# A decoder layer on one core: the attention's first unit of scores placed in front of the last projected block

## The chip, the core and the metric

The kernel runs on one core of a Trainium2 chip. The metric is the device time of one execution in microseconds (us); lower is better. The kernel before takes 804.1 us, the median of three executions (803.87 to 805.67). A difference of some 0.2% (1.6 us) is about what the measurement can tell from none.

## What is computed

A decoder layer in float32 on x[4, 512, 512] with a context[4, 512, 512], 16 heads of 32:

```python
x = x + self_attention(layernorm(x))        # causal; q, k, v, o projections with biases
x = x + cross_attention(layernorm(x), ctx, ctx)   # causal; no projections: keys = values = context
h = layernorm(x)
x = x + relu(h @ W_up.T) @ W_down.T + sum(softmax(top2(h @ W_gate.T))) * (h @ W_expert)
```

Both attentions are softmax(q k^T / sqrt(32)) v under a causal mask. The softmax subtracts each row's maximum, so the kernel forms the scores twice: once to find the maxima, and once, transposed and with the maxima subtracted, for the exponentials.

## The kernel before, in words

**Stages.** The four batches b = 0 to 3 are worked one after the other. Each has a self attention (stages s0 to s3), a cross attention (c0 to c3) and a feed-forward part. The 16 heads are four groups g of four heads. Besides, each attention stage has *fill*: projections of a neighbouring part, which give TensorE something to do while the maxima are found. A fill matmul (128x128 weights, 512 columns, float32) is two TensorE instructions. Four of them make a block of 128 rows or columns of a result. The fill is queries, keys and values of batch 0 in s0; up and down projections of batches 0 and 1 in s1 and s2; queries and keys of the next batch in c0, c1 and c2, with the expert blocks of batch 0 behind them in c1; expert blocks of batch 1 and two up blocks of batch 2 in s3; four down blocks of batch 2 in c3.

**Maxima.** `with_maxima` (L905) emits ten units of narrow score matmuls (32 rows of weights, `Attention.maxima`, L293), here called M1 to M10. Each unit fills two PSUM pairs, ScalarE copies them out (L304, two copies of 1024 columns), POOL masks the diagonal (L312), VectorE reduces to maxima (L324), and after the last unit of a group `split` (L341 to L350, VectorE) cuts the maxima into three bfloat16 parts. Between the units come the fill matmuls, shared out by a running due; a unit's VectorE jobs are emitted one by one behind the fill matmuls of the next gap. `rows` (L352) transposes a group's parts on TensorE (tiles `mt`, L361) and copies them to SBUF (`mrow`, L367); in cross attention `masked_sums` and `masked` (tiles `mb`, `ct`) do the like for fully masked keys.

**Scores and values.** `attend` (L954) then emits ten units of transposed scores (L405, with the maxima subtracted by the bfloat16 matmuls of L416), here sc0 to sc9: (g,0), then (g,3)+(g,1), then (g,2)+(g+1,2), then (g+1,0), then (g+1,3)+(g+1,1), twice. Each takes two PSUM pairs; ScalarE takes the exponential (L439, two of 1024 columns), POOL masks (L447), VectorE adds up the sums of the softmax (L552), and `values` multiplies with v (L482, tiles `pv`, one PSUM pair for the whole of a group). In the kernel before, `values` of the first unit (pv0) comes behind sc2. Behind sc3 come the transposes of the remaining maxima (`mt_..._both`).

**What sets the order.** The order of instructions on TensorE, VectorE, ScalarE and POOL is the order in which the code emits them (`tc.manual_schedule`). Each engine works its queue in order. PSUM is one pool of four pairs (L63 to L67); a new tile takes a pair once the reader of its last tile has released it. So a late reader on ScalarE or VectorE stops TensorE at the next tile that takes this pair.

**Evacuations.** Two blocks share a PSUM pair and are evacuated together, in one VectorE add of 1024 columns for v (`value`, L685) and down (`down`, L843), two weighted adds for the expert blocks (`weigh`, L867, each followed by a store on SP's queue), one ScalarE relu for up, and two ScalarE activations for queries and keys (`query_key`).

## Time and profile before

| what | us |
| --- | --- |
| median of three executions | 804.1 |
| their range | 803.87 to 805.67 |
| span of the profiled execution, first to last instruction | 803.7 |
| TensorE busy | 794.0 |
| VectorE busy | 565.9 |
| ScalarE busy | 395.2 |
| POOL busy | 339.6 |
| TensorE waits named in the trace, all | 5.7 |

The four named waits of TensorE are 2.4 us for the first layernorm, 1.5 us for the identity matrix, and 0.9 us each in the scores of the self and of the cross attentions (four times 0.2 us each), for exponentials. TensorE's queue can stand still for longer than these rows say: matmuls are pipelined, their recorded ends are modelled, and a stop shows as a longer distance between two starts. So the starts in the timeline are what to read. Busy times are averages over stages that differ: VectorE has long idle stretches at the start of a stage and is full at its end.

### The profile page before, as it was taken

What the parts mean: (1) busy time and instruction counts of PE and PEld (TensorE: products, weight loads), DVE (VectorE), ACT (ScalarE), POOL (GpSimd) and SP (SyncE); (2) the same over time, 40 slices, a digit from 0 to 9 for tenths busy, and PEclk for the clock granted to TensorE, in tenths of its full rate; (3) what the DMA queues carried; (4) which work ended last, traced back from release to release, by engine and by line L of the source; (5) the groups of instructions that cost most, each with busy time, mean ns of one, the idle gap of its engine ahead of it and who ended that gap; (6) DMA issues with size and microseconds to landing.
All of it is one profiled execution on the core that took longest, in us unless ns stands there. A gap on an engine that the chain in (4) does not pass through costs nothing.

```text
span 803.7 us, 13927 instructions
## 1 busy us (share of the span) xinstructions
PE 794.0 (99%) x5588; PEld 378.9 (47%) x5592; DVE 565.9 (70%) x963; ACT 395.2 (49%) x448; POOL 339.6 (42%) x523
## 2 busy tenths in 40 slices
PE   8999999999999999999999999999999999999998
PEld 6444454444444454444544455444444444444544
DVE  2378855889679854678867786588959766988512
ACT  2457516871456615567055742687156833674110
POOL 3434612564234732257332482256423652475100
PEclk9999999999999999999999999999999999999999
DMA  9710000001010000021100000000102000000101
GB/s 301 275 28 1 2 1 1 2 27 54 1 27 2 2 0 1 2 78 55 53 14 14 1 2 0 1 1 2 53 28 80 2 1 1 1 2 1 53 1 52
DMA packets 15282, 24.51 MB, mean 30 GB/s; under 512 B 2033, under 2 KB 5361, under 8 KB 15217
## 3 DMA queue, kind: packets, MB, share of 16 engines
q1 hardware_dynamic: 14496, 22.96, 8.6%
q8 instruction: 44, 0.72, 0.4%
q10 hardware_dynamic: 720, 0.66, 0.2%
q14 instruction: 22, 0.17, 0.1%
HBM read 19.42 MB, written 4.19 MB: 29 GB/s over the span
## 4 chain that ended last, share of the span: by engine, by line
PE 95%; ACT 2%; issue 1%; DMA 1%; DVE 0%; ACTq 0%
PE pm_qk L241 14%; PE pm_d L229 7%; PE pm_u L241 7%; PE pm_v L229 7%; PE pm_o L725 7%; PE pm_e L229 7%; PE pv_c L482 6%; PE pv_s L482 6%; PE sm_c L293 6%; PE sm_s L293 6%; PE sc_s L405 5%; PE sc_c L405 5%; PE sc_s L416 1%; PE sc_c L416 1%; PE tp_a L255 1%
## 5 line engine op out<-in xcount | busy, mean ns | idle before, releaser
L324 DVE TENSOR_REDUCE nm_s<-s_s 128x2 f32<-128x1024 f32 (+3 forms) x128 | 96.9, 810 | 34.7 <-POOL s_s L312 34.7
L324 DVE TENSOR_REDUCE nm_c<-s_c 128x2 f32<-128x1024 f32 (+3 forms) x128 | 95.8, 810 | 31.0 <-POOL s_c L312 31.0
L304 ACT COPY s_s<-sm_s 128x1024 f32<-128x1024 f32 x80 | 77.1, 1015 | 70.7 <-PE sm_s L293 36.7
L304 ACT COPY s_c<-sm_c 128x1024 f32<-128x1024 f32 x80 | 77.1, 1016 | 35.9 <-PE sm_c L293 16.2
L312 POOL TENSOR_SCALAR_AFFINE_SELECT s_c<-s_c 128x512 f32<-128x512 f32 (+1 forms) x80 | 43.9, 550 | 100.4 <-ACT s_c L304 100.4
L312 POOL TENSOR_SCALAR_AFFINE_SELECT s_s<-s_s 128x512 f32<-128x512 f32 (+1 forms) x80 | 43.8, 551 | 94.4 <-ACT s_s L304 94.4
L552 DVE TENSOR_TENSOR sum_s<-sum_s,pt_s 128x256 f32<-128x256 f32 (+2 forms) x72 | 59.9, 897 | 15.4 <-PE pv_s L482 15.4
L439 ACT ACTIVATE pt_c<-sc_c 128x1024 f32<-128x1024 f32 x64 | 61.7, 1031 | 18.1 <-PE sc_c L416 10.1
L447 POOL TENSOR_SCALAR_AFFINE_SELECT pt_c<-pt_c 128x512 f32<-128x512 f32 (+1 forms) x64 | 52.9, 833 | 20.7 <-ACT pt_c L439 20.2
L229 PE MATMUL pm_d<-wdown_sb,hT 128*128 128x512 f32 x128 | 61.5, 611 | 0.0
L241 PE MATMUL pm_qk<-xnT,wk_sb 128*128 128x512 f32 x128 | 61.0, 606 | 0.0
L241 PE MATMUL pm_u<-fT,wup_sb 128*128 128x512 f32 x128 | 59.3, 605 | 0.0
L439 ACT ACTIVATE pt_s<-sc_s 128x1024 f32<-128x1024 f32 x56 | 53.9, 1030 | 10.5 <-POOL pt_s L447 5.5
L229 PE MATMUL pm_v<-wv_sb,xnT 128*128 128x512 f32 x128 | 58.8, 600 | 0.0
L725 PE MATMUL pm_o<-wo_sb,oT_s 128*128 128x512 f32 x128 | 57.8, 596 | 0.0
L405 PE MATMUL sc_c<-cqT,ckT 32*128 32x384 f32 (+3 forms) x512 | 56.4, 464 | 0.9 <-ACT sum_c L439 0.9
L241 PE MATMUL pm_qk<-xnT,wq_sb 128*128 128x512 f32 x120 | 56.7, 605 | 0.0
L229 PE MATMUL pm_e<-wexp_sb,fT 128*128 128x512 f32 x120 | 56.3, 604 | 0.0
L447 POOL TENSOR_SCALAR_AFFINE_SELECT pt_s<-pt_s 128x512 f32<-128x512 f32 (+1 forms) x56 | 48.0, 865 | 16.9 <-ACT pt_s L439 16.2
L405 PE MATMUL sc_s<-qT,kT 32*128 32x128 f32 (+3 forms) x512 | 54.1, 464 | 0.9 <-ACT sum_s L439 0.9
L293 PE MATMUL sm_c<-ckT,cqT 32*128 32x512 f32 (+3 forms) x512 | 47.5, 460 | 0.0
L293 PE MATMUL sm_s<-kT,qT 32*128 32x512 f32 (+3 forms) x512 | 47.0, 461 | 0.0
(171 smaller groups left out, 1268.1 us busy)
## 6 DMA issues: line engine op xcount, KB each, us to landing
cv<-in_ctx_dram SPq DMA_DIRECT2D x16, 256.0 KB, 4.4
out_dram<-x SPq DMA_DIRECT2D x15, 256.0 KB, 2.0
xin<-in_x_dram SPq DMA_DIRECT2D x12, 256.0 KB, 2.8
x<-in_x_dram SPq DMA_DIRECT2D x12, 256.0 KB, 4.2
wq_sb<-in_wq_dram SPq DMA_DIRECT2D x2, 512.0 KB, 6.7
wk_sb<-in_wk_dram SPq DMA_DIRECT2D x2, 512.0 KB, 7.7
wv_sb<-in_wv_dram SPq DMA_DIRECT2D x1, 1024.0 KB, 7.8
wo_sb<-in_wo_dram SPq DMA_DIRECT2D x1, 1024.0 KB, 9.5
```

What stands on the lines that cost most here:

```text
L229: nc.tensor.matmul(pm, lhsT=lhs_t[:, c, t * P : (t + 1) * P], rhs=w[:, c, :], start=(c == 0), stop=(c == NC - 1),)
L241: nc.tensor.matmul(pm, lhsT=w[:, c, f * P : (f + 1) * P], rhs=rhs_t[:, c, :], start=(c == 0), stop=(c == NC - 1),)
L293: nc.tensor.matmul(scs[r // 2][:, r % 2, c : c + (i + 1) * P], lhsT=self.q_t[h, g, i * P : (i + 1) * P], rhs=self.k_t[h, g, : (i + 1) * P] ...
L304: nc.scalar.copy(s, scs[n])
L312: nc.gpsimd.affine_select(out=diagonal, in_=diagonal, compare_op=ALU.is_ge, fill=NEG, base=0, pattern=[[0, 2], [0, len(pieces)], [-1, P]], ...
L324: nc.vector.tensor_reduce(self.nm[g][:, i, 2 * n : 2 * n + 2], made[n][:, :, c : c + (i + 1) * P], axis=AX.X, op=ALU.max, negate=True,)
L405: nc.tensor.matmul(scs[r // 2][:, r % 2, c : c + S - j * P], lhsT=self.k_t[h, g, j * P : (j + 1) * P], rhs=self.q_t[h, g, j * P :], start= ...
L439: nc.scalar.activation(pt, scs[n], AF.Exp)
L447: nc.gpsimd.affine_select(out=diagonal, in_=diagonal, compare_op=ALU.is_ge, fill=0.0, base=0, pattern=[[0, 2], [0, len(pieces)], [1, P]], ...
L482: nc.tensor.matmul(pv[r * HD : (r + 1) * HD, u, j * P :], lhsT=ones if u else self.v[:, j, h * HD : (h + 1) * HD], rhs=pts[r // 2][:, r % ...
L552: nc.vector.tensor_tensor(to, to, pts[n][:, :, c : c + S - j * P], ALU.add)
L725: nc.tensor.matmul(pms[t // 2][:, t % 2, :], lhsT=a.out[:, c, t * P : (t + 1) * P], rhs=wo_sb[:, c, :], start=(c == 0), stop=(c == NC - 1),)
```

## The change

`with_maxima` keeps the last block of the fill apart (`last`). Its other blocks are shared out over the gaps between the ten maxima units (`merge=1`: nine gaps, so that nothing stands behind M10; `merge=0`: ten). Then it emits sc0, the first unit of scores, then the four matmuls of the last block, between them the VectorE jobs of M10, and then hands over to `attend`, which goes on with sc1. In c0, c1, c2, c3 and s3 (`merge=1`) sc0 follows M10 directly; in s0, s1 and s2 two or three fill matmuls still stand between. In s0 six fill matmuls instead of two lead, so that M1 has what it needs. `attend` multiplies the values of sc0 behind sc1 instead of behind sc2. The last block and the one before no longer share a PSUM pair in the stages' fills: each gets its own pair and is evacuated by itself. In c0 and c2 only the last key block gets a pair of its own, and its queries are evacuated ahead of it. In the stages where the copy of the third group's maxima stood in the last gap (c0, c1, c2) it now stands behind the second matmul of the last block.

```diff
     def query_key(e):
-        b, made = e.b, {}
+        b, made, apart = e.b, {}, (NC - 1,) if e.b % 2 else ()
...
         def query(f):
             made[f] = pair(f"pm_qk{b}_{f}")
             yield from project_t(made[f][:, 0, :], wq_sb, e.xn_t, f)
+            if f in apart:
+                out_query(f)
...
         def key(f):
-            yield from project_t(made[f][:, 1, :], wk_sb, e.xn_t, f)
-            out(f)
+            if f in apart:
+                pm = pair(f"pm_k{b}_{f}")[:, 0, :]
+            else:
+                pm = made[f][:, 1, :]
+            yield from project_t(pm, wk_sb, e.xn_t, f)
             nc.scalar.activation(
-                e.k_t[:, f, :], made[f][:, 1, :], AF.Identity, bias=bk_sb[:, f : f + 1]
-            )
+                e.k_t[:, f, :], pm, AF.Identity, bias=bk_sb[:, f : f + 1]
+            )
+            if f not in apart:
+                out_query(f)
...
         def one(t):
+            if b == 0 and t >= NT - 2:
+                pm = pair(f"pm_v{b}_{t}")[:, 0, :]
+                yield from project(pm, e.xn_t, wv_sb, t)
+                nc.vector.tensor_tensor(e.v[:, t, :], pm, bv_sb, ALU.add)
+                return
...
+            if b == B - 2 and f < 2:
+                pm = pair(f"pm_u{b}_{f}")[:, 0, :]
+                yield from project_t(pm, wup_sb, f_t, f)
+                nc.scalar.activation(made["h"][:, f, :], pm, AF.Relu)
+                return
...
         def down(t):
+            if t >= NT - 2 and b < B - 1:
+                pm = pair(f"pm_d{b}_{t}")[:, 0, :]
+                yield from project(pm, made["h"], wdown_sb, t)
+                if b == B - 2:
+                    aside(f"d{b}_{t}", t, pm)
+                else:
+                    nc.vector.tensor_tensor(e.x[:, t, :], pm, e.x[:, t, :], ALU.add)
+                return
...
         def expert(t):
...
+            if b == 0 and t >= NT - 2:
+                pm = pair(f"pm_e{b}_{t}")[:, 0, :]
+                yield from project(pm, f_t, wexp_sb, t)
+                weigh(t, pm, slice(0, D), nc.sync)
                 return
...
-    def with_maxima(steps, a, first=0, norms=()):
+    def with_maxima(steps, a, first=0, norms=(), merge=1):
...
+        fill, last = matmuls(steps[first:-1]), matmuls(steps[-1:])
+        total = sum(1 if step.__name__ in ("share", "gate") else NC for step in steps[first:-1])
+        early = total + NC >= 2 * len(units)
+
+        lead = 6 if first else 0
...
+        late = {3: NC - 1} if early else {3: 2, 5: NC - 1}
...
-            due += (total - lead) / len(units)
+            due += (total - lead) / (len(units) - merge)
...
-                if n == len(units) - 1 and k == count - (2 if count > 4 else 1):
-                    if total >= 2 * len(units):
-                        if a.cross:
-                            a.rows(2)[0](nc.scalar.copy)
-                    else:
-                        late = {3: 2, 5: NC - 1}
...
+        begun = [a.scores([(0, 0)])]
+        for k in range(NC):
+            next(last)
+            if k == 1 and a.cross and early:
+                a.rows(2)[0](nc.scalar.copy)
+            run(jobs[:1])
+            jobs = jobs[1:]
+        for _ in last:
+            pass
         run(jobs)
-        return late
+        return begun, late

-    def attend(a, late):
+    def attend(a, begun, late):
...
-        waiting, held, todo = [], [], []
+        waiting, held, todo = list(begun), [], []
...
-        for n, pieces in enumerate(units):
+        for n, pieces in enumerate(units[1:], 1):
             waiting.append(a.scores(pieces))
...
-            if len(waiting) > 2:
+            if n == 1 or n > 2:
                 values()
...
-            late = with_maxima(between_self, sa, skip, norms)
+            begun, late = with_maxima(between_self, sa, skip, norms, int(not more))
...
-            late = with_maxima(steps[3:], ca)
+            begun, late = with_maxima(steps[3:], ca)
```

More of the change, by code (lines that the diff above doesn't have):

```diff
@@ L638, in query, with out_query @@
             yield from project_t(made[f][:, 0, :], wq_sb, e.xn_t, f)
+            if f in apart:
+                out_query(f)
         def key(f):
-            yield from project_t(made[f][:, 1, :], wk_sb, e.xn_t, f)
-            out(f)
-        def out(f):
+            if f in apart:
[3 more added lines that the diff above has]
+            yield from project_t(pm, wk_sb, e.xn_t, f)
             nc.scalar.activation(
-                e.k_t[:, f, :], made[f][:, 1, :], AF.Identity, bias=bk_sb[:, f : f + 1]
+                e.k_t[:, f, :], pm, AF.Identity, bias=bk_sb[:, f : f + 1]
             )
+            if f not in apart:
+                out_query(f)
+        def out_query(f):
             nc.scalar.activation(
@@ L837, in down @@
             yield from project(made["d"][:, t % 2, :], made["h"], wdown_sb, t)
-            if t == NT - 1 and b == B - 2:
-                for n in range(2):
-                    aside(f"d{b}_{n}", t - 1 + n, made["d"][:, n, :])
-            elif t % 2 == 1:
+            if t % 2 == 1:
                 both = e.x[:, t - 1 : t + 1, :]
@@ L847, in expert @@
                 yield from expert_parts(t)
+                return
+            if b == 0 and t >= NT - 2:
+                pm = pair(f"pm_e{b}_{t}")[:, 0, :]
+                yield from project(pm, f_t, wexp_sb, t)
+                weigh(t, pm, slice(0, D), nc.sync)
                 return
@@ L903, in matmuls @@
             yield
-    def with_maxima(steps, a, first=0, norms=()):
-        norms = list(norms)
-        run(steps[:first])
-        fill = matmuls(steps[first:])
-        total = sum(1 if step.__name__ in ("share", "gate") else NC for step in steps[first:])
+    def with_maxima(steps, a, first=0, norms=(), merge=1):
         units = []
@@ L916, in with_maxima @@
             units += [u for k in (g, g + 1) for u in ([(k, 2), (k, 0)], [(k, NT - 1)])]
-        lead = 2 if first else 0
+        norms = list(norms)
+        run(steps[:first])
+        fill, last = matmuls(steps[first:-1]), matmuls(steps[-1:])
+        total = sum(1 if step.__name__ in ("share", "gate") else NC for step in steps[first:-1])
+        early = total + NC >= 2 * len(units)
+        lead = 6 if first else 0
         for _ in range(lead):
             next(fill)
-        done, due, jobs, late = lead, float(lead), [], {3: NC - 1}
+        late = {3: NC - 1} if early else {3: 2, 5: NC - 1}
+        done, due, jobs = lead, float(lead), []
         todo = []
@@ L1017, in decoder_layer @@
                 after, norms, turns = norm_in(b + 1)
-            late = with_maxima(between_self, sa, skip, norms)
+            begun, late = with_maxima(between_self, sa, skip, norms, int(not more))
             if b == B - 1:
                 e.x = load_x(b)
-            attend(sa, late)
+            attend(sa, begun, late)
             if b > 0:
@@ L1031, in decoder_layer @@
             ca.e, ca.out = e, e.beh_t
-            late = with_maxima(steps[3:], ca)
+            begun, late = with_maxima(steps[3:], ca)
             if b + 2 < B:
                 after.x = load_x(b + 1)
-            attend(ca, late)
+            attend(ca, begun, late)
             if more:
```

## The prediction

> **What bounds the kernel.** I read the page first, engines and then the chain of waits:

> ```profile
> PE 794.0 (99%) x5588; PEld 378.9 (47%) x5592; DVE 565.9 (70%) x963; ACT 395.2 (49%) x448; POOL 339.6 (42%) x523
> ...
> PE 95%; ACT 2%; issue 1%; DMA 1%; DVE 0%; ACTq 0%
> ```

> TensorE is nearly the whole chain, its granted clock is 9 (full) in every slice of the page, and the change keeps the number of its matmuls. So the only time to win is the few per cent in which TensorE's queue stands still, and the only time to lose is a new stop in it, or a change between the wide projections (128x128) and the narrow scores (32x128). Next I read TensorE's timeline where the first self attention begins (s0; columns: start, duration, instructions):

> ```profile
> 62.86 1.14 PE L293 MATMUL sm_s<-kT,qT 32*128 32x512 f32 x8
> 63.93 2.84 PE L229 MATMUL pm_v<-wv_sb,xnT 128*128 128x512 f32 x6
> 66.70 1.14 PE L405 MATMUL sc_s<-qT,kT 32*128 32x512 f32 x8
> ...
> 67.88 1.35 PE L405 MATMUL sc_s<-qT,kT 32*128 32x128 f32 x16
> ...
> 69.16 0.70 PE L405 MATMUL sc_s<-qT,kT 32*128 32x256 f32 x4
> 70.07 0.92 PE L405 MATMUL sc_s<-qT,kT 32*128 32x256 f32 x10 [0.21 <-ACT sum_s L439]
> ...
> 71.35 1.07 PE L482 MATMUL pv_s<-sum_s,v 128*32 128x512 f32 x8
> 72.35 1.17 PE L405 MATMUL sc_s<-qT,kT 32*128 32x512 f32 x6
> ...
> 74.10 0.62 PE L361 MATMUL mt_s_both<-identb,parts 128*128 128x128 bf16 x8
> ```

> M10 at 62.86, three fills (2.77), then sc0, sc1, sc2. sc2 starts at 69.16, stops after four matmuls and goes on at 70.07, when ScalarE's exponentials of sc0 have freed a PSUM pair. sc2 thus takes 2.19 (69.16 to 71.35) where the same shape undisturbed takes 1.38 (84.02 to 85.40); sc3 takes 1.75 (72.35 to 74.10) where 0.97 plus about 0.3 for the change to the transposes would do. Together about **1.3 us of stop** in a stage; in c0 about 1.7 (157.35 to 164.88). Eight stages of it are 11 to 12 us: all that the change can win. Then VectorE in the same stretch, because the new waits point there:

> ```profile
> 62.21 2.34 DVE L324 TENSOR_REDUCE nm_s<-s_s 128x2 f32<-128x1024 f32 x2
> ...
> 66.81 1.23 DVE L685 TENSOR_TENSOR v<-pm_v,bv_sb 128x1024 f32<-128x1024 f32 x1
> 67.95 1.27 DVE L324 TENSOR_REDUCE nm_s<-s_s 128x2 f32<-128x768 f32 x2
> 69.14 0.74 DVE L212 TENSOR_SCALAR xn_a<-xin,mv_a,rs_a 128x512 f32<-128x512 f32 x1
> 69.79 2.33 DVE L324 TENSOR_REDUCE nm_s<-s_s 128x2 f32<-128x1024 f32 x2
> ...
> 73.57 0.23 DVE L350 TENSOR_TENSOR parts<-rest_s,parts 128x16 bf16<-128x16 f32 x1
> ```

> VectorE is about 7 us behind TensorE: M10's scores were done at 63.9, their reductions run from 69.79, and the split of the last group ends at 73.80. The queue is solid from 57.1 on. In before nothing that TensorE needs early stands at its end.

> **The change, part by part.** (1) *Order.* Four projection matmuls (4 x 0.86 = 3.44 straight, 3.63 with the change of shape) stand between sc0 and sc1, so that sc0's two exponentials (1.94, row 68.08) run beside them. sc1 and the first half of sc2 then find their pairs. That is the gain. (2) *A new back-to-back.* values(sc0) now comes before sc2, so sc2 and sc3 follow each other and pv0 keeps a pair; sc3's second tile waits for the exponential of sc2's first tile: 0.97, with 0.2 until ScalarE starts (67.88 to 68.08) and as much until the scores are whole, less 0.5 for sc3's first tile that runs meanwhile. The trace has no such pair of units; the ends are 0.5 and 1.4, and I take a **0.95 stop** in every stage. So at best 1.3 - 0.95, some 0.35, is won, and in c0/c2 0.4 to 0.7. (3) *Changes of shape.* A unit between fills costs about 0.2 for each entry and exit (two fills take 1.92, where 2 x 0.86 is 1.72). In s0, s1, s2 M10 and sc0 stay apart, with one more pair of changes: +0.4 each, part of it hidden in the stop before. In the five stages in one visit the number of changes stays. (4) *Halved evacuations.* An add over 1024 columns takes 1.22 (L685), over 512 0.68 (L740): splitting adds 0.14 of VectorE, and frees the pair of block 2 earlier. (5) *A new wait at the end of a queue.* The last block has its own PSUM pair. With four pairs the turn comes round: by the waits of the built program sc2's first tile takes the pair of the last block. In s0, s1, s2 and c1 VectorE evacuates that block, and its add stands behind M10's reductions and the split. In c0, c2 (L648), s3 (relu) and c3 (the copy aside) it is ScalarE, which takes it in time (0.58 to 0.69). Behind the add on VectorE stand the L552 sums, and on TensorE sc2 holds up all else, as it works in order. The rest costs nothing: in c1 the stores on SP's queue are as many as before (one of 256 KB after each weighted add, median 2.0 us to land by the page) and no matmul waits for them; in c3 POOL's two put-off adds are the same two; ScalarE's copy of the third group's maxima (0.58) moves behind sc0's exponentials into a queue that has 1.9 free (354.54). If these covers failed, the copy alone would delay sc1's exponentials by 0.6.

> *s0.* Three fewer matmuls stand before M10: 62.86 - 2.58 = 60.3; M10 1.07, two fills 1.92: sc0 at 63.3; to the fills 1.18, last block 3.64: sc1 at 68.1; +1.46: pv0 69.6; +1.0: sc2 wants to start at **70.6**. VectorE: M8's reductions can start at 61.6 (0.6 earlier, the row idle at 57.1 closes), and the rest is 11.6 in before (62.21 to 73.80) - 1.23 + 0.68: split done at about 72.7, last add at **73.4**. sc2 stops for 2.8. Then 1.38, sc3's 0.97 + 0.95: the transposes at 76.7 instead of 74.10: **+2.6**. If the add came in time it would be -0.15.

> *s1, s2.* VectorE's rows, before:

> ```profile
> 250.05 1.22 DVE L843 TENSOR_TENSOR x<-pm_d,x 128x1024 f32<-128x1024 f32 x1 [1.25 <-PE pm_d L229]
> ...
> 253.03 2.33 DVE L324 TENSOR_REDUCE nm_s<-s_s 128x2 f32<-128x1024 f32 x2
> ```

> The 1.25 of waiting goes, as block 2 is done sooner, and M10 comes 3.4 earlier (four fewer matmuls before it). By the same steps sc0 is at 246.5, sc2 wants 253.8; VectorE's split ends at 253.7 to 254.6 (257.04 in before, less 1.25, less 0.5 to 0.7 for the halved add, less up to 0.9 of older idle time) and the add 0.7 later, 254.4 to 255.3. Stop 0.6 to 1.5; I take 1.2, transposes near 258.3 against 257.34: **+0.9** each; with the add in time -0.2.

> *c1.* As many matmuls stand before M10; sc0 follows at 350.6. Its second tile needs the pair of block 2, whose weighted add (0.70, half of the row of 1.41 at 354.31) now stands behind the split that ends at 350.99: done at 351.7, a stop of 1.3 where there is none now. Transposes near 362.7 against 361.83: **+0.9**; without the stop -0.4.

> *c0, c2.* sc0 follows M10 at 153.35, sc1 at 158.6, transposes 164.5 to 164.9 against 164.88: **-0.2** each.

> *s3, c3.* Two fewer matmuls before M10. If TensorE alone sets the pace, M10 is 1.7 earlier and the way from M10 to the transposes is 12.5 instead of 10.4 (s3) or 11.2 (c3): +0.4 (s3), -0.4 (c3). But c3's fills are as short as one matmul and VectorE is nearly full there; M10 itself is stretched to 1.98 (702.45) by its PSUM pair. If M10 can't move, it is +2.1 (s3) or +1.3 (c3). VectorE's slack in s3 is larger; I take 0 and **+0.3**, with the ends -0.4 and +1.5 for both.

> The sum: 2.6 + 0.9 + 0.9 + 0.9 - 0.4 + 0 + 0.3 = **+5.2 us**. The profiled span is 803.7, the median of the runs 804.1; the difference I carry over: **809.3**. With every cover in place: -0.15 - 0.4 - 0.4 - 0.8 - 0.8 = -2.5, so 801.6. With every end the other way (VectorE not ahead in s0: 3.3; s1, s2 1.5 each; c1 1.3; s3, c3 1.5 each) +10.6.

> [...]

> **Rivals.** *A, forecast:* the last block's add at the end of VectorE's queue holds sc2 in s0 to s2, and c1's sc0: 806 to 812. For: VectorE's solid rows. Against: the lag in s1/s2 is only about 1 us longer than the cover. *B, the other side:* the add comes in time, as VectorE gets its maxima earlier than I counted. In s0 VectorE must gain 2.8 us, in s1/s2 1.2, in c1 1.3; then only part 2's stop remains and the eight stages give -2.5: **801.6**, faster. For: M10's scores are 3 to 4 us earlier, and VectorE has free time ahead of them (3.32 us idle before 50.23); where ScalarE's copies set the start of the reductions, all moves ahead. Against: that idle time was ended by the transposes of the first group, which stay at about 50. *C, even:* the stops are there, but in s1, s2 and c1 no longer than what (1) gives: +2.6 - 0.2 - 0.2 - 0.4 - 0.8 = about +1 to -1: **804 to 805**. *D, worse:* c3 and s3 are held by VectorE and M10 doesn't move: **812 to 815**. *E,* that the change does not do what it says: sc0 is in front of the last block in the instruction lists, so I give it nothing.

> **The numbers.** A 0.63, B 0.18, C 0.13, D 0.06. Less than 0.2% (1.6 us) is about what a measurement of this kernel can tell from no change. Faster by more: B and little else, 0.19. Within: C, 0.13. Slower: A and D, 0.68. The likeliest is A at 809.3, its own range 806 to 812. For 8 in 10 I leave out D and the far end of B: 802.0 to 812.0.

> **What would show it.** In the profile after: in s0, between pv0 and sc2, TensorE idle or stretched for about 2.8 us, ended by VectorE's add of v, and the transposes near 76.7; in s1 and s2 the same of 1 us with the add of pm_d; in c1 sc0 stretched by 1.3. In every stage a stop of about 0.95 inside sc3, ended by the exponential of sc2. In c0 the transposes near 164.7. I am wrong if sc2 starts right behind pv0 in s0 (then B), if sc3 shows no stop (then the gain is up to 7 us larger), or if the loss is in c3 or s3.

## The result, and the profile after

The changed kernel takes 811.88 us (median of four executions, 810.52 to 813.52) against 804.03 us of the kernel before on the same chip; the ratio is 1.0092, with a 95% interval of 1.0075 to 1.0109. It is slower by 7.4 us by that ratio, by 7.9 us by the medians. The forecast was 809.3, its range 802.0 to 812.0.

The page of the changed kernel: TensorE does the same 5588 matmuls, and the span grows from 803.7 to 811.9.

```profile
PE 798.5 (98%) x5588; PEld 378.1 (47%) x5592; DVE 561.8 (69%) x966; ACT 396.4 (49%) x449; POOL 337.8 (42%) x523
```

TensorE's waits in the changed kernel (us in total, times, longest) name who held it:

```profile
PE sc_s L405 <- DVE v L691: 2.4, 1, 2.4
PE tp_a L255 <- DVE xn_a L212: 1.9, 1, 1.9
PE sc_c L405 <- ACT pt_c L439: 1.5, 4, 0.4
...
PE sc_s L405 <- ACT pt_s L439: 1.0, 3, 0.4
PE sm_s L293 <- ACT qT L655: 0.5, 1, 0.5
PE sc_c L405 <- DVE x L894: 0.2, 1, 0.2
```

The first row is the last block's add in s0, the last one the weighted add in c1, the `pt` rows are the stop between sc2 and sc3. TensorE's timeline of s0 in the changed kernel, to be laid beside the one in the prediction:

```profile
63.99 1.14 PE L405 MATMUL sc_s<-qT,kT 32*128 32x512 f32 x8
...
65.27 3.70 PE L229 MATMUL pm_v<-wv_sb,xnT 128*128 128x512 f32 x8
68.91 1.15 PE L405 MATMUL sc_s<-qT,kT 32*128 32x128 f32 x16
...
70.20 1.07 PE L482 MATMUL pv_s<-sum_s,v 128*32 128x512 f32 x8
73.63 1.62 PE L405 MATMUL sc_s<-qT,kT 32*128 32x256 f32 x16 [2.36 <-DVE v L691]
...
75.44 2.43 PE L405 MATMUL sc_s<-qT,kT 32*128 32x512 f32 x6
...
78.45 0.62 PE L361 MATMUL mt_s_both<-identb,parts 128*128 128x128 bf16 x8
```

pv0 ends at 71.27 and nothing runs until 73.63. VectorE in the same stretch shows why: the add of the last block of v stands behind M10's reductions and the split.

```profile
68.90 2.34 DVE L324 TENSOR_REDUCE nm_s<-s_s 128x2 f32<-128x1024 f32 x2
...
72.33 0.69 DVE L350 TENSOR_TENSOR parts<-rest_s,parts 128x16 bf16<-128x16 f32 x1
72.90 0.68 DVE L691 TENSOR_TENSOR v<-pm_v,bv_sb 128x512 f32<-128x512 f32 x1
```

**Where the 8 us came from.** In each stage I took the start of the last transposes of maxima in `attend` (the `mt` rows, 74.10 and 78.45 in s0), subtracted the same row of the kernel before, and from that the difference of the stage before. s0 is counted from the start of M1, less the 3.44 us of the four matmuls that now stand ahead of it. (In e4, e8 and e9 nothing is taken off, as s0 is that of the kernel before.) This leaves out the time up to M1, which differs by up to 2.2 us between profiled executions (the first layernorm ends TensorE's wait after 0.5 to 2.45 us) and also moves the totals. e5 has no row: its one profiled execution ran at a mean clock of 0.947, where the others have 0.996 to 1.000. Differences to the kernel before in us:

| kernel | s0 | c0 | s1 | c1 | s2 | c2 | s3 | c3 | ratio of times (95%) |
| --- | --- | --- | --- | --- | --- | --- | --- | --- | --- |
| changed | +4.40 | +1.44 | -0.22 | +1.17 | -0.22 | +1.43 | +0.19 | -0.01 | 1.0092 (1.0075 to 1.0109) |
| e1 jobs behind the add | +1.02 | +1.44 | -0.29 | +1.17 | -0.28 | +1.43 | +0.18 | -0.01 | 1.0053 (1.0041 to 1.0066) |
| e2 values as before | +4.79 | +1.02 | -0.32 | +0.62 | -0.32 | +0.89 | -0.40 | -0.33 | 1.0066 (1.0054 to 1.0079) |
| e3 both | +0.43 | +0.85 | -0.88 | +0.58 | -0.87 | +0.84 | -0.40 | -0.33 | 0.9990 (0.9981 to 0.9999) |
| e4 s0 as before | +0.01 | +1.48 | -0.23 | +1.18 | -0.23 | +1.43 | +0.18 | -0.01 | 1.0039 (1.0026 to 1.0053) |
| e6 fill and weigh | +0.43 | 0.00 | -0.88 | +3.50 | -0.88 | 0.00 | -0.40 | -0.32 | 1.0012 (1.0003 to 1.0020) |
| e7 busy in the stop | +3.38 | +1.43 | -0.22 | +1.17 | -0.22 | +1.43 | +0.19 | -0.02 | 1.0079 (1.0065 to 1.0092) |
| e8 all but s0 | +0.01 | +0.05 | -0.88 | +3.54 | -0.87 | -0.01 | -0.40 | -0.33 | 0.9989 (0.9980 to 0.9999) |
| e9 five stages | +0.01 | +0.02 | -0.88 | -0.54 | -0.88 | -0.05 | -0.40 | -0.31 | 0.9962 (0.9949 to 0.9975) |
| e10 apart everywhere | +0.44 | +1.71 | -0.88 | -0.03 | -0.88 | +1.72 | +1.12 | +0.93 | 1.0048 (1.0034 to 1.0062) |
| e11 together everywhere | +0.34 | +0.85 | +0.45 | +0.58 | +0.44 | +0.86 | -0.40 | -0.31 | 1.0023 (1.0013 to 1.0033) |
| e12 paired evacuations | +0.43 | +2.00 | -0.88 | +1.16 | -1.07 | +1.99 | +0.87 | +0.36 | 1.0055 (1.0041 to 1.0068) |

A stage that an edit leaves alone repeats to about 0.05 us from run to run (s0 as before: +0.01 three times; the other seven stages in the changed kernel, e4 and e7), so the table resolves more than the totals do. The expectations of e5, e6, e8 and e9 quote figures of the e3 row that are 0.2 to 0.3 higher in the cross stages and as much lower in s1, s2 and s3; by the definition above the figures are those of the table. Half of the loss is in s0, most of the rest in c0, c1 and c2; s1, s2, s3 and c3 are even.

### The profile page after: what moved, and what is told of

Same layout as the page of the kernel before. It is cut to its first block, busy times and chain, and to the rows that moved or that the text cites. A ratio compares the mean times of both kernels' runs of the same rounds, so it can differ in the third digit from the quotient of the medians.

```text
span 811.9 us, 13931 instructions
## 1 busy us (share of the span) xinstructions
PE 798.5 (98%) x5588; PEld 378.1 (47%) x5592; DVE 561.8 (69%) x966; ACT 396.4 (49%) x449; POOL 337.8 (42%) x523
## 5 line engine op out<-in xcount | busy, mean ns | idle before, releaser
L324 DVE TENSOR_REDUCE nm_s<-s_s 128x2 f32<-128x1024 f32 (+3 forms) x128 | 97.0, 810 | 36.6 <-POOL s_s L312 36.4
L324 DVE TENSOR_REDUCE nm_c<-s_c 128x2 f32<-128x1024 f32 (+3 forms) x128 | 95.7, 811 | 31.0 <-POOL s_c L312 31.0
L552 DVE TENSOR_TENSOR sum_s<-sum_s,pt_s 128x256 f32<-128x256 f32 (+2 forms) x72 | 59.5, 887 | 26.5 <-PE pv_s L482 21.9
L439 ACT ACTIVATE pt_c<-sc_c 128x1024 f32<-128x1024 f32 x64 | 62.0, 1021 | 24.5 <-PE sc_c L416 14.5
L439 ACT ACTIVATE pt_s<-sc_s 128x1024 f32<-128x1024 f32 x56 | 54.3, 1021 | 25.4 <-PE sc_s L416 14.7
L447 POOL TENSOR_SCALAR_AFFINE_SELECT pt_s<-pt_s 128x512 f32<-128x512 f32 (+1 forms) x56 | 50.3, 908 | 34.4 <-ACT pt_s L439 33.8
L229 PE MATMUL pm_d<-wdown_sb,hT 128*128 128x512 f32 x128 | 60.9, 609 | 0.0
L405 PE MATMUL sc_c<-cqT,ckT 32*128 32x384 f32 (+3 forms) x512 | 57.5, 460 | 1.8 <-ACT pt_c L439 1.5
L229 PE MATMUL pm_v<-wv_sb,xnT 128*128 128x512 f32 x128 | 58.9, 600 | 0.0
L405 PE MATMUL sc_s<-qT,kT 32*128 32x128 f32 (+3 forms) x512 | 54.4, 469 | 3.5 <-DVE v L691 2.4
L229 PE MATMUL pm_e<-wexp_sb,fT 128*128 128x512 f32 x120 | 56.5, 604 | 0.0
L241 PE MATMUL pm_qk<-xnT,wk_sb 128*128 128x512 f32 x112 | 53.6, 605 | 0.0
L293 PE MATMUL sm_c<-ckT,cqT 32*128 32x512 f32 (+3 forms) x512 | 50.5, 460 | 0.0
L293 PE MATMUL sm_s<-kT,qT 32*128 32x512 f32 (+3 forms) x512 | 46.5, 461 | 0.5 <-ACT qT L655 0.5
```

The lines of the kernel that those rows point to most:

```text
L229: nc.tensor.matmul(pm, lhsT=lhs_t[:, c, t * P : (t + 1) * P], rhs=w[:, c, :], start=(c == 0), stop=(c == NC - 1),)
L241: nc.tensor.matmul(pm, lhsT=w[:, c, f * P : (f + 1) * P], rhs=rhs_t[:, c, :], start=(c == 0), stop=(c == NC - 1),)
L293: nc.tensor.matmul(scs[r // 2][:, r % 2, c : c + (i + 1) * P], lhsT=self.q_t[h, g, i * P : (i + 1) * P], rhs=self.k_t[h, g, : (i + 1) * P] ...
L324: nc.vector.tensor_reduce(self.nm[g][:, i, 2 * n : 2 * n + 2], made[n][:, :, c : c + (i + 1) * P], axis=AX.X, op=ALU.max, negate=True,)
L405: nc.tensor.matmul(scs[r // 2][:, r % 2, c : c + S - j * P], lhsT=self.k_t[h, g, j * P : (j + 1) * P], rhs=self.q_t[h, g, j * P :], start= ...
L439: nc.scalar.activation(pt, scs[n], AF.Exp)
```

## The experiments

Theory Q was the forecast's: the last block's evacuation stands at the end of VectorE's queue and holds the PSUM pair of sc2. Rival B: the order sc2, sc3 back to back costs. Rival F, formed from the table: four matmuls kept back leave too little fill between the maxima in c0 and c2.

**e1: M10's VectorE jobs behind the last block.**

```diff
         for k in range(NC):
             next(last)
...
-            run(jobs[:1])
-            jobs = jobs[1:]
         for _ in last:
             pass
         run(jobs)
```

> As the changed kernel, but the VectorE jobs of M10 (two to four reductions and the split) are emitted behind the last block instead of between its matmuls, so the block's evacuation stands ahead of them in VectorE's queue. Theory Q (VectorE's queue holds the last block's PSUM pair): in s0 the add of v is done at about 69.6 instead of 73.5, sc2 starts directly behind pv0 (71.2 instead of 73.6), and the slower granted clock behind the stop (0.62 and 0.74 in the 5.4 us after it) goes too: 3 to 4 us less, all in s0; 808 to 809. Rival B (the back-to-back of sc2 and sc3 is what costs): the stop of 1.4 in sc3 stays in each of eight stages, the time stays at 811 to 812. Rival F (too little fill between the maxima): no change either, 811 to 812.

Measured: 809.51 us, ratio 1.0053. The time is half a microsecond above what Theory Q gave, the place is right: s0 falls by 3.38, and no other stage moves by more than 0.07. VectorE's timeline of e1 in s0 now has the add first:

```profile
69.12 0.69 DVE L691 TENSOR_TENSOR v<-pm_v,bv_sb 128x512 f32<-128x512 f32 x1
69.73 2.33 DVE L324 TENSOR_REDUCE nm_s<-s_s 128x2 f32<-128x1024 f32 x2
```

And in TensorE's timeline of e1 sc2 follows pv0 directly:

```profile
70.31 1.06 PE L482 MATMUL pv_s<-sum_s,v 128*32 128x512 f32 x8
71.31 1.31 PE L405 MATMUL sc_s<-qT,kT 32*128 32x256 f32 x16
...
73.91 0.70 PE L405 MATMUL sc_s<-qT,kT 32*128 32x512 f32 x2 [0.38 <-ACT pt_s L439]
...
75.18 0.62 PE L361 MATMUL mt_s_both<-identb,parts 128*128 128x128 bf16 x8
```

Theory Q holds for s0. The row of 73.91 is the stop that stays: sc3's second tile waits for an exponential of sc2.

**e2: the values of sc0 behind sc2, as before.**

```diff
-            if n == 1 or n > 2:
+            if len(waiting) > 2:
                 values()
```

> As the changed kernel, but the values of sc0 come behind sc2 again, as in the kernel before; sc2 and sc3 are no longer back to back. Theory Q: s0 keeps its stop, as VectorE's add comes at 73.5 either way; little changes, 811 to 812. Rival B: the stop of 1.4 in sc3 shrinks to about 0.4 in each of eight stages, 6 to 8 us less: 804 to 806, and half of that if the stop only moves to sc2's second tile. Rival F: 811 to 812.

Measured: 809.86 us, ratio 1.0066. Neither number came. By stages it is 0.1 to 0.6 shorter everywhere but in s0, where it is 0.4 longer. The stop of sc3 goes, but sc2's second tile now asks for the last block's pair 1 us earlier: TensorE waits 2.94 for the add of v in s0, and 0.7 and 0.6 for that of `pm_d` in s1 and s2.

**e3: both edits.**

> Both edits of the two runs before together. Theory Q alone: as with the first edit, 808 to 809. Rival B alone: as with the second, 804 to 806. If the two are separate terms they add up: 811.9 - 3.5 - 6 = about 802.5, faster than the kernel before (804.0).

Measured: 804.04 us, ratio 0.9990: level with the kernel before by the bound of 0.2%. The stages sum to 8.0 us less than in the changed kernel, where the two edits alone give 3.5 and 2.2: the second shows its full worth only when the first wait is gone. s1 and s2 fall from -0.22 to -0.88 and -0.87. Against e1, which has the first edit alone, e3 is shorter by 0.58 or 0.59 in every stage but c3 (0.32). That is what values behind sc1, with sc2 and sc3 back to back, costs more than the old order: 4.4 us in all, so Rival B of these experiments is right too. In TensorE's waits of e3 two rows of the attentions are left, the 0.5 for qT in s0 and the 0.2 for the weighted add in c1.

**e4: s0 as in the kernel before.** Order and evacuations of s0 are those of the kernel before, the rest is changed.

> As the changed kernel, but s0 keeps the order and the paired evacuations of the kernel before; the other seven stages are changed. By the stages' starts in the two traces s0 lost 4.3 us of the 8.1, c0 and c2 1.5 each, c1 1.2, the others 0.2 or less. Theory Q: s0's loss is its own and goes whole: 807.5 to 808. Rival F (c0 and c2 lose by thin fills): the same here; c0, c1, c2 keep +1.5, +1.2, +1.5. If the loss moves to the next stage instead, 810 to 812.

Measured: 808.05 us, ratio 1.0039. The 4.4 us of s0 go whole, c0, c1 and c2 keep theirs (+1.48, +1.18, +1.43). What s0 loses is not handed on to the other stages.

**e5: the change in s1, s2 and s3 only**, with both edits of e3.

> The change only in s1, s2 and s3, where the traces put a gain once M10's VectorE jobs stand behind the last block and the values of sc0 come behind sc2 (both edits are in); s0 and the cross stages as in the kernel before. By the stages' starts in the run with both edits, s1 and s2 gain 1.1 each and s3 0.6. If the stages are independent: 2.8 us less than the kernel before, 0.35%, 801 to 802 where it takes 804. If a gain in one stage is given back in the next, within 0.1% of before.

Measured: ratio 0.9967 (0.9955 to 0.9978), 2.7 us faster than the kernel before (1.8 to 3.6 by the interval). The three stages of e3 sum to 2.2, which lies inside.

**e6: fill and weigh.** e3 with two edits more. In c0 and c2 the gaps with one matmul come first; in c1 M8's reductions and the split come behind the weighted add.

```diff
-            due += (total - lead) / (len(units) - merge)
+            if a.name in ("c0", "c2"):
+                due += 1 if n < 2 else 2 if n < 9 else 0
+            else:
+                due += (total - lead) / (len(units) - merge)
...
             for k in range(count):
...
+                if a.name == "c1" and n == 8:
+                    continue
                 run(jobs[:1])
```

> As the run with both edits, all stages changed, and two more edits: in c0 and c2 the two gaps with a single fill matmul are the first two instead of the third and the seventh; in c1 the reductions of M8 and the split stand behind the weighted add of the last but one expert block. Theory F (a gap of one fill matmul is shorter than ScalarE's two copies of 1.93, where ScalarE also has the evacuations of keys, queries and ct to do): c0 and c2 fall from +1.1 each against before to about -0.2. Theory Q for c1: its sc0 no longer waits for the add, +0.8 becomes -0.3 or so. Together 3 to 3.5 us less than with both edits alone: ratio to before about 0.995 to 0.996. If c0's and c2's loss comes from the order behind M10 and not from the fill, they stay at +1.1.

Measured: 805.47 us, ratio 1.0012, longer than e3. The half on c0 and c2 came: +0.85 and +0.84 become 0.00, so the place of the thin gaps is the whole of what e3 still lost there. In e3 M8 of c0 stands behind a gap of one matmul and is stretched; ScalarE works without a break from 143.41 to 148.89 beside it. In e6 the same unit has a gap of two ahead of it and is not. The first line is of e3, the second of e6:

```profile
144.53 1.98 PE L293 MATMUL sm_c<-ckT,cqT 32*128 32x512 f32 x8
```

```profile
145.82 1.14 PE L293 MATMUL sm_c<-ckT,cqT 32*128 32x512 f32 x8
```

The half on c1 failed: +0.58 became +3.50. sc0 no longer waited, but the split was now late, and the transposes of the third group, in the middle of the last block, waited for it. A wait took the place of another, as TensorE's timeline of e6 shows:

```profile
350.57 1.98 PE L229 MATMUL pm_e<-wexp_sb,fT 128*128 128x512 f32 x4
354.84 0.40 PE L361 MATMUL mt_c<-identb,parts 128*128 128x128 bf16 x4 [2.29 <-DVE parts L350]
```

**e7: work in the stop.** The changed kernel with two matmuls more in s0, written to the half of pv0's pair that is overwritten later.

```diff
+            if n == 1 and a.name == "s0":
+                for c in range(2):
+                    nc.tensor.matmul(
+                        a.pv[0][:, 1, :],
+                        lhsT=e.xn_t[:, c, :P],
+                        rhs=wv_sb[:, c, :],
+                        start=(c == 0),
+                        stop=(c == 1),
+                    )
```

> As the changed kernel, plus two matmuls of 128x128 by 512 float32 (four instructions, 1.7 us) in s0 between pv0 and sc2, in the stop of 2.4 us; they write a half of pv0's PSUM pair that is overwritten later, so nothing that counts is changed. If the granted clock falls because TensorE stood idle, the clock behind the stop stays at 1.00 instead of 0.62 and 0.74, sc2 to the transposes takes 3.9 instead of 4.8, and s0 is about 0.9 us shorter although it does more: 811 against 811.9. If the clock has nothing to do with it, s0 is the same or up to 0.2 longer, as VectorE's add still ends at 73.5.

Measured: 810.54 us, ratio 1.0079; in the profiled execution s0 is 1.02 shorter than in the changed kernel although it does 1.7 us more work. The wait left is 0.45, and sc2 to the transposes takes 3.79 instead of 4.82. The windows of the changed kernel (columns: window, its length, busy time of PE, PEld, DVE, ACT and POOL with counts, then the granted clock, then DMA share and GB/s) show the cost that this takes away:

```profile
73.00:74.00 1.00, 0.37 (x8) 0.36 (x12) 1.00 (x4) 0.00 (x0) 0.00 (x0) 1.00 0.00 0
74.00:75.00 1.00, 1.00 (x16) 0.71 (x12) 1.00 (x2) 0.00 (x0) 0.00 (x0) 0.58 0.06 16
75.00:76.00 1.00, 1.00 (x14) 0.75 (x8) 0.98 (x2) 0.26 (x1) 0.00 (x0) 0.50 0.00 0
76.00:77.00 1.00, 1.00 (x6) 0.18 (x6) 0.00 (x0) 1.00 (x2) 0.17 (x1) 0.50 0.02 8
77.00:78.00 1.00, 1.00 (x8) 0.42 (x6) 0.50 (x1) 0.68 (x1) 0.72 (x2) 0.71 0.00 0
```

The granted clock falls to 0.50 some 0.5 us after work has begun again at 73.63, for some 3.4 us. The windows of e7, with work in the stop (its sc2 starts at 71.53), stay at 1.00:

```profile
70.00:73.60 3.60, 3.15 (x31) 1.44 (x29) 3.57 (x7) 0.77 (x2) 0.64 (x1) 1.00 0.02 5
73.60:76.00 2.40, 2.10 (x22) 0.98 (x24) 1.02 (x3) 2.07 (x3) 1.58 (x2) 1.00 0.01 3
```

That the slow clock costs 1.0 us here is shown; e1, which has no stop, needs 3.87 from sc2 to the transposes. That the added work is what kept the clock up is the likely reading of one trace; the last section tells why it is not certain.

**e8: all four edits, s0 as before.**

> All four edits (M10's jobs behind the last block, values of sc0 behind sc2, the thin gaps first in c0 and c2, the weighted add of c1 ahead of M8's reductions), with s0 as in the kernel before. If the terms add: s1 and s2 -1.1 each, s3 -0.6, c0, c2 and c1 about -0.2 each, c3 0: 3.5 us less than before, ratio 0.9955 to 0.9965, about 800.5 to 801. If the cross stages' losses are of another kind, 803 to 804.

Measured: 803.07 us, ratio 0.9989, which misses the 800.5 to 801 expected. Every stage shows what it had in e4 or e6, but c1 carries the failed edit (+3.54).

**e9: five stages.** The change in s1, c1, s2, s3 and c3, with both edits of e3; in c1 the weighted add stands between M8's reductions and the split.

```diff
+                if a.name == "c1" and n == 8 and k == 2:
+                    continue
                 run(jobs[:1])
```

> The change in s1, c1, s2, s3 and c3 only, with M10's jobs behind the last block and the values of sc0 behind sc2; in c1 the weighted add of the last but one expert block now stands between M8's reductions and the split (not ahead of the reductions, where the split and with it the transposes of the third group came 2.3 us late). Theory Q: sc0 in c1 waits about 1 us less than with both edits alone, c1 falls from +0.8 to 0 or -0.3 against before; s1 and s2 -1.1 each, s3 -0.6, c3 -0.1: 3.0 us less than the kernel before, ratio about 0.996. If the add only moves the wait to the transposes again, c1 is +1 or more and the ratio 0.998.

Measured: 801.19 us against 804.62, ratio 0.9962: faster than both kernels. c1 goes from +0.58 in e3 to -0.54, with one VectorE instruction in another place; the eight stages sum to -3.0, the ratio gives -3.1. VectorE's timeline of e9 has it behind the reductions; the split begins at 348.23:

```profile
343.81 3.85 DVE L324 TENSOR_REDUCE nm_c<-s_c 128x2 f32<-128x256 f32 x5
347.57 0.74 DVE L894 SCALAR_TENSOR_TENSOR x<-pm_e,rw,x 128x512 f32<-128x512 f32 x1
348.23 0.17 DVE L345 TENSOR_TENSOR nm_c<-nm_c,nfloor 128x16 f32<-128x16 f32 x1
```

**e10: M10 and sc0 apart everywhere** (e3 with `merge` 0 in all stages).

> As the run with both edits, all stages changed, but no stage has M10 and sc0 in one visit: the fills are shared out over ten gaps, so one or two stand between M10 and sc0 in c0, c1, c2, c3 and s3 too. Two more changes between the shapes in each of these five stages cost 0.4 each, 2.1 in all; and the thinner gaps (16 matmuls over ten gaps in c0 and c2) cost more where ScalarE's copies set the pace. Theory F: 2 to 4 us more than with both edits, ratio to before 1.002 to 1.004. If the changes of shape are hidden in waits: 0 to 1 us more, or less where M10's copies then free the pair of sc0 in time.

Measured: 808.25 us, ratio 1.0048, about 4 us more than e3: the upper end of Theory F, and a little over its ratio. It is not the changes of shape alone: c1 even gains 0.6 (sc0 asks for its pair later), c0 and c2 lose 0.9 each, c3 1.3, and s3 loses 1.5, of which 1.4 is a new wait of its first up block for an expert block's weighted add. So the number came for partly another reason.

**e11: together everywhere** (e3 with `merge` 1 in all stages).

> As the run with both edits, but all eight stages have M10 and sc0 in one visit. By the changes of shape alone s0, s1 and s2 gain 0.4 each, 1.2 us less than with both edits. Theory Q: in s1 and s2 sc0's second tile then takes the pair of the last but one down block directly behind M10, and its add stands behind M8's reductions, the split and M9's first ones in VectorE's queue: a stop of 1.5 to 2.5 in each, and about as much in s0; with a stop over 2 us also a slower clock behind it. 4 to 8 us more than with both edits, ratio 1.004 to 1.009.

Measured: 806.56 us, ratio 1.0023. s1 and s2 lose 1.3 each, as sc0's second tile waits for the add of `pm_d`; the place is right, the size is below the 1.5 to 2.5 expected, and s0, where as much was expected, gains 0.1. The number (1.004 to 1.009) missed.

**e12: paired evacuations** (e3 with the evacuations of the kernel before).

> As the run with both edits, but with the evacuations of the kernel before: the last two blocks of each stage share a PSUM pair and are evacuated together behind the last one. Theory Q: with the shared pair, sc0's second tile in c1 takes M10's pair and no longer waits for a weighted add: c1 -0.5 or so; the evacuation behind the last block is 1.22 instead of 0.68 on VectorE, hidden beside sc1. In c0 and c2 kT and qT are both evacuated behind the last block, 1.3 instead of 0.6 on ScalarE, which delays sc1's exponentials by 0.6. Together within 1 us of the run with both edits, ratio 0.998 to 1.000. If the halved evacuations are what makes the order possible, the stops come back: 3 us or more longer, ratio over 1.003.

Measured: 808.58 us, ratio 1.0055. The main expectation missed. s0, s1 and s2 don't need the halved evacuations, but c0 and c2 lose 1.15 each, c1 0.6, s3 1.3 and c3 0.7: with one pair for both blocks sc0's second tile asks for a pair of M10, right behind M10, and waits for ScalarE's copy. TensorE's timeline of e12 in s3:

```profile
618.71 1.02 PE L405 MATMUL sc_s<-qT,kT 32*128 32x512 f32 x4
620.03 0.70 PE L405 MATMUL sc_s<-qT,kT 32*128 32x512 f32 x2 [0.30 <-ACT s_s L304]
```

So the halved evacuations belong to the stages in one visit, where they free a pair at the right moment.

## Why the prediction was right, and where its terms were off

The mechanism, the sign and the place came: the last block's add holds sc2 in s0, and e1 takes that away alone. That the total came too is in part luck. The sum was 5.2, the stages show 8.2: s0 was 1.8 and c0 and c2 were 1.6 each too small, s1 and s2 were 1.1 each too large, and 811.88 lies 0.12 inside the range.

By the table the 8.2 are: 3.5 for the add behind M10's jobs (the changed kernel to e1, 3.4 of it in s0), 4.4 for the back-to-back of sc2 and sc3 (e1 to e3), 1.7 for the thin gaps of c0 and c2 (e3 to e6), 1.1 for the weighted add in c1 (e3 to e9), less 2.6 that the rest of the change gains. The edits were measured one on top of the other, not each alone.

*s0, forecast +2.6, measured +4.4.* The add was done at 73.5, forecast 73.4. The stop was 2.4, forecast 2.8, as sc2 wanted to start at 71.2 and not at 70.6: M6's scores waited for ScalarE's qT, which the sum did not have (0.46 by the wait's row; 0.8 by the starts, 2.03 from M6 to the fill behind it, 1.21 in the kernel before). What was left out altogether is the clock: 1.0 us. The prediction read the page's 9 as full speed in every slice. A 9 is 90% or more and a slice some 20 us, so a short fall does not show there. The kernel before has one, behind TensorE's wait of 2.45 us for the first layernorm, in a window of its trace (columns as above):

```profile
9.00:10.00 1.00, 1.00 (x7) 1.00 (x6) 0.93 (x3) 0.00 (x0) 0.47 (x1) 0.50 1.08 380
```

*s1, s2, forecast +0.9 each, measured -0.22.* The step "add 0.7 later, 254.4 to 255.3" failed. Its sum was also added up wrongly: 257.04 less 1.25, less 0.5 to 0.7, less up to 0.9 is 254.2 to 255.3 for the split and 0.7 more for the add. In the changed kernel s1 stands 5.79 later (the transposes of c0), and the add ended at 259.06, which is 253.3 in the times of the forecast:

```profile
258.38 0.68 DVE L858 TENSOR_TENSOR x<-pm_d,x 128x512 f32<-128x512 f32 x1
```

pv0 started at 257.97 and sc2 at 259.12, 1.15 later, where e1 has 1.00 in s0: 0.15 of a stop, and e1 gains 0.07 and 0.06 in s1 and s2. M10's reductions began 3.6 earlier than in the kernel before (255.21, less 5.79, against 253.03), and the split took 0.9 (257.58 to 258.50), where I had taken the 1.64 of the kernel before with its stretched casts (255.40 to 257.04). The forecast for the add in time was -0.2, and that is what came.

*c1, forecast +0.9, measured +1.17.* The wait of sc0's second tile was right in place and about right in size: 1.3 forecast, and e9, which removes it, has 1.1 less than e3.

*c0, c2, forecast -0.2 each, measured +1.4.* The term that failed is "sc0 follows M10 at 153.35": M10 of c0 came 0.39 earlier, counted from the transposes of s0 (79.65 against 80.04), instead of 1.7. The way from M10 to the transposes was 12.57, forecast 12.1 to 12.5. Of the two matmuls that left the gaps ahead of M10 most was not saved, as a unit behind a gap of one waits while ScalarE is busy with copies and evacuations (M8, in e6 above); e6 gives back 0.85 in each stage and e3 the other 0.6. I had bounded this for s3 and c3 and not for the two stages where it happened; those came out at +0.19 and -0.01.

*The stop inside sc3.* Forecast 0.95. sc2 to the transposes takes 3.8 to 3.9 in s1 and c1 of the changed kernel, where 1.38 + 0.97 + 0.3 would do: the stop is about 1.2, in the bounds of 0.5 to 1.4.

*Rivals.* B, the faster one, needed the add in time everywhere. e1 has it in time in s0, s1 and s2 and still loses 4.7 us by the stages. With the thin gaps (1.7) and c1's wait (1.1) taken off, a loss of 1.9 is left where B had a gain of 2.5. C was right for s1 and s2 alone. Of D, c3 and s3 held by VectorE, nothing came.

What stays open: why s0 keeps +0.43 in e3 and e6. M6's wait on qT is still there in both and is larger than that by the starts, but no run took it away.

## What to carry to other kernels

When a block of matmuls is moved behind a new consumer of PSUM, look at what its evacuation is queued behind, not at how long it takes: here an add of 0.68 us held the chain for 2.4, and moving it ahead of six instructions (two reductions and four of the split), without a change of the work, was worth 3.4 us in the profiled execution, 1.0 of it by the clock. Fill that is kept back for a later gap has to be missing somewhere; here the first two gaps could spare it, where the third and the seventh could not (0.85 us in each of two stages); I read this as ScalarE having less to copy at the start, which no run separates. And an edit like this is decided by stage: with both edits the same code gains 0.9 us in two stages and 0.3 to 0.4 in two, and loses 0.4 to 0.9 in four, so the version to keep has it where it gains (e9, 0.38% faster than before).

## What the runs showed of the hardware

| run, place | stop, us | work again at | clock at 0.50, from and to |
| --- | --- | --- | --- |
| changed kernel, s0 | 2.36 | 73.63 | 74.16, 77.58 |
| e6, c1 | 2.29 | 354.84 | 355.96, 359.38 |
| e2, s0 | 2.94 (1.80 of it in the windows) | 71.80 | 73.16, 76.56 |
| changed kernel, first layernorm | 1.90 | 8.44 | 9.32, 12.72 |
| kernel before, first layernorm | 2.45 | 8.58 | 8.46, 11.88 |

In the attentions the fall came 0.5 to 1.4 us after work had begun again. The windows read behind three shorter stops are at 1.00: 0.45 in s0 of e7, and inside sc3 0.30 in s1 and 0.38 in c1 of the changed kernel. One fall of 3.4 us at a half takes 0.002 off the mean clock of the span, an estimate from the table and the span of 811.9. By that the profiled executions of e9, with 1.79 us at the wait for the first layernorm, and of e10, with 1.39 in s3, have no whole fall: their mean clocks are 1.000. That of e8, with 1.70 at the first layernorm and 2.29 in c1, is at 0.998.

The fall does not come in every execution. The four executions of the changed kernel have mean clocks of 0.996, 0.995, 0.999 and 0.999 and times of 813.52, 812.76, 811.00 and 810.52: by the same estimate no whole fall can have happened in the last two. Of the twelve of e8, seven are at 1.000 (802.75 to 803.08) and five at 0.998 (804.42 to 805.31), and the profiled one is of the five. What decides it no run here shows. For the same reason e7 alone can't settle that the added work kept the clock up, though none of its six executions is below 0.998.

Two of VectorE's small operations of the split (128x16, L348 to L350, medians of 0.19 to 0.23 us in the changed kernel) took 1.19 and 1.33 in c1 of e6, and 0.55 and 0.69 in s0 of the changed kernel, while POOL was at work; no run tells whether POOL is the cause.
